# Earlier places for head projections and a dispatch, a root in place of a power, and first rows fetched before their weights, in a two-layer transformer kernel

## The chip, the cores and the metric

The kernel runs on one core of one Trainium2 chip. The metric is the device time of one execution in microseconds (us); lower is better. Before the change three runs took 674.36, 676.66 and 676.97 us, so the median is 676.66 us.

## The reference, cut to what matters

The input is 2048 tokens (8 sequences of 256) of 128 channels, all float32. Six blocks follow one another, each with a residual:

```python
x = x + 0.5 * L0_ffn(layernorm(x))   # mixture of experts, stage f=0
x = x + L0_attn(layernorm(x))        # 16 heads of 8 channels
x = x + 0.5 * L0_ffn(layernorm(x))   # the same mixture, stage f=1
x = x + 0.5 * L1_ffn(layernorm(x))   # channel mix
x = x + L1_attn(layernorm(x))        # gated long convolution
x = x + 0.5 * L1_ffn(layernorm(x))   # channel mix again

def L0_ffn(s):
    h = rmsnorm(s @ W_in.T)
    logits = h @ Wr.T                       # 8 experts
    idx = top_k(logits + expert_bias, 2)    # two experts for each token
    gates = softmax(logits[idx])
    ...
    oe = rmsnorm((silu(h @ Wg[e].T) * (h @ Wu[e].T)) @ Wd[e].T)
    out = sum of gates * oe over the token's two experts
    return rmsnorm(out) @ W_out.T
```

## The kernel before

Tokens lie in four chunks `xs[0..3]` of 512 (four tiles of 128 rows). SP issues plain DMAs, POOL issues the indirect ones.

**A dispatch** sends a group of tokens to its experts. For f=1 there are five, `LATE = (0, 4), (4, 4), (8, 4), (12, 2), (14, 2)` (first tile, number of tiles), numbered 0 to 4 here. Its pieces are `turned` (transpose, PE, and a copy, ACT), `product` twice (`half0`, `half1`: projection to h and logits, then row sums of squares), `measured` (variance of x, DVE), `normed` (1 over the root, `ri`), `logits`, `scaled` (rows of h to `hrow`, ACT), `choice` 0 and 1 (the two best experts, chains of small DVE operations), `places` (a running count by matmuls against a triangle, `prank`, which gives each row its place `posi`), and `rows`: one indirect DMA a tile and choice, from POOL, that writes 128 rows of `hrow` into `hs` in DRAM. Four-tile dispatches have eight such DMAs, two-tile ones four. In f=1 `normed` lets POOL compute the power -0.5 (`power_of`, L144); in f=0 ACT takes the root and DVE the reciprocal (L349, L350).

**The table.** After the last dispatch DVE works out from the counts which expert each of 24 tile turns belongs to (`table`), SP and ACT queue eight DMAs that write zeros behind each expert's rows (`zeros`, L514), and SP then fetches for each turn the expert's weights (`w_f`, L544, 832 KB) and the rows (`hst_f`, L550, 129 KB for 256 rows). Each fetch is preceded by a load of a register from the table. The fetch of rows waits for all writes of `hs`. PE then runs for each turn the transposes of the rows (`pht`), `pg` and `pu` (L566) and, a turn later, `py` (L589). Four weight buffers rotate.

**Attention** stands between the two mixtures. It runs in steps s = 0 to 34, each with two places "a" and "b": s is a sequence and a group of four heads (eight steps a chunk). In each place PE computes weights (`ps`, L910) for one earlier step side by side with scores (`pm`, L893) for the new one; ACT takes the exponentials (`es`), DVE the maxima (`m`). Other work is hung into the places by hand, `at(step, place, pieces)`: the combination of f=0's output for chunk n, its layer norm (`norm_sums`, `norm_rows`), the transposes (`turn_rows`, `pxn_a`), the projections to q and k (`to_heads`, part 0 and part 1, `pqk`, copied to `qkc`), the values, the ends of earlier sequences (`turn_back`, `turn_heads`, `out_heads`), and the dispatches of f=1. `to_heads` part 1 also queues one DMA to DRAM (`heads<-qkc`) and four that bring q and k back with the heads spread over partitions (`qk<-heads`); chunk n's scores begin at step 8n. These side jobs share one PSUM bank, `sa`, so each waits for the reader of the one before. PE, DVE, ACT and SP keep the program's order; POOL's order comes from the scheduler.

Of the kernel before, what the change touches and what calls it, by code (L numbers as in the profile page):

```python
# [11 lines left out]
AF = mybir.ActivationFunctionType  # L12
# [5 lines left out]
B, S, D = 8, 256, 128  # L18
# [4 lines left out]
E, DFF = 8, 512  # L23
# [7 lines left out]
I32 = mybir.dt.int32  # L31
# [8 lines left out]
TURNS = [t for i in range(7) for t in (2 * i, 2 * i + 1, NPAIR + i)] + [14, NPAIR + 7, NPAIR + 8]  # L40
# [6 lines left out]
WALL = 3 * DFF + D  # L47
# [4 lines left out]
def macaron_kernel(ctx: ExitStack, tc: tile.TileContext, a: dict, out: bass.AP):  # L52
    nc = tc.nc
# [32 lines left out]
    rms_eps = const.tile([P, 1], F32, tag="rms_eps", name="rms_eps")  # L86
# [10 lines left out]
    def pack(name, widths, rows=P):  # L97

        t = const.tile([rows, sum(widths)], F32, tag=name, name=name)
        nc.sync.dma_start(t, a[name])  # L100
        cuts, o = [], 0
        for w in widths:
            cuts.append(t[:, o : o + w])
            o += w
        return cuts

    load_x(0)
    win, wr_t, inw, eb, tri, slot, base, order, tokid = pack(
        "pack1", [D, E, 1, E, P, 2, E, E, NCH * TPC * 2]
    )  # L110
    tokid = tokid.rearrange("p (t k) -> p t k", k=2).bitcast(I32)
# [4 lines left out]
    zero = const.tile([P, 2 * ROW], F32, tag="zero", name="zero")  # L116
    nc.vector.memset(zero, 0.0)
    warm = const.tile([P, 1], F32, tag="warm", name="warm")
    nc.scalar.activation(warm, rms_eps, AF.Sqrt)

    hs = tc.dram_tile([HS_ROWS, ROW], F32, name="hs")
    (tabc,) = pack("pack2", [TABLE])
# [176 lines left out]
    def dispatch(f, i, parts, mp):  # L299

        t0, nt = parts[i]
        n = f"f{f}_{i}"
        st = {}
        x = xs[t0 // TPC][:, t0 % TPC : t0 % TPC + nt, :]
        hrow = hrows[t0 // TPC][:, t0 % TPC : t0 % TPC + nt]
        slots = slice(t0, t0 + nt)
# [38 lines left out]
        def normed():  # L345
            ri = small.tile([P, nt], F32, tag="ri", name=f"ri_{n}")
            nc.vector.scalar_tensor_tensor(ri, st["ss"], 1.0 / D, st["z"], ALU.mult, ALU.add)  # L347
            if f == 0:
                nc.scalar.activation(ri, ri, AF.Sqrt)  # L349
                nc.vector.reciprocal(ri, ri)  # L350
                nc.vector.tensor_copy(hrow[:, :, :, D].bitcast(I32), tokid[:, slots])
            else:
                power_of(ri, ri, mhalf.to_broadcast([P, nt]))
            st["ri"] = ri
# [75 lines left out]
        halves, choices = ([partial(p, i) for i in range(2)] for p in (product, choice))  # L430
# [101 lines left out]
    def experts(f, tab, far, y2, mp, pieces):  # L532

        SP = mybir.EngineType.SP
        hst, w, ht, hg = {}, {}, {}, {}
# [4 lines left out]
        def fetch_weights(t):  # L540
            n = f"f{f}_{t}"
            e = nc.values_load(tab[0:1, 1, t : t + 1], engines=[SP], min_val=0, max_val=E - 1)
            w[t] = mp.tile([P, WALL], F32, tag="w", name=f"w_{n}", bufs=4)
            nc.sync.dma_start(w[t], a["wall"][bass.ds(e, 1), :, :].rearrange("o p f -> p (o f)"))  # L544

        def fetch_rows(t):
            n, m = f"f{f}_{t}", blocks(t)
            row = nc.values_load(tab[0:1, 0, t : t + 1], engines=[SP], min_val=1, max_val=HS_ROWS - TT)
            hst[t] = mp.tile([P, 2, ROW], F32, tag="hst", name=f"hst_{n}", bufs=4)[:, 0:m]
            nc.sync.dma_start(hst[t], hs[bass.ds(row, m * P), :].rearrange("(s p) c -> p s c", p=P))  # L550
# [67 lines left out]
                tc.add_to_no_dep_group(f"y2{f}", ins.ins)  # L618

        for t in TURNS[:3]:  # L620
            fetch_weights(t)
            fetch_rows(t)
        turn_rows(TURNS[0])
        for i, t in enumerate(TURNS):
            sg = gate(t)
# [107 lines left out]
    def heads(hp):  # L733
# [26 lines left out]
        def attention(mixing, leaving, filter_ends):  # L760
# [5 lines left out]
            with tc.tile_pool(name="at2", bufs=2, reuse_waits="tile") as a2:  # L766
# [206 lines left out]
                def at(s, h, *pieces):  # L973
                    places_[s, h] += pieces
# [7 lines left out]
                for n in range(1, NCH):  # L982
                    sums, added, turned, produced, update = mixing[n + 1]
                    o = 8 * n - 8
                    if n == 1:
                        at(0, "b", sums)
                        at(1, "b", added)
                        o += 1
                    else:
                        at(o - 1, "b", sums)  # L990
                        at(o, "b", added)
                    at(o + 1, "a", turned)
                    at(o + 1, "b", produced)
                    at(o + 2, "a", update)
                    at(o + 2, "b", partial(norm_sums, n))
                    at(o + 3, "a", partial(norm_rows, n))
                    if n == 1:
                        at(3, "b", seq1[4])
                        o -= 1
                    at(o + 4, "b", partial(turn_rows, n))  # L1000
                    at(o + 5, "a", partial(to_heads, n, part=0))
                    at(o + 5, "b", partial(to_heads, n, part=1))
                    at(o + 8, "a", partial(values, n))
                for b in range(B - 1):
                    o = 4 * b
# [8 lines left out]
                for c in range(2):  # L1014
                    o = 8 * c + 8
                    turned, half0, half1, measured, normed_, logits, scaled, *choices, places, rows = leaving[c]
                    at(o + 4, "a", turned)
                    at(o + 4, "b", measured)
                    at(o + 6, "a", half0)
                    at(o + 8, "b", half1)  # L1020
                    at(o + 9, "a", normed_)
                    at(o + 9, "b", logits, choices[0])
                    at(o + 10, "b", partial(scaled, [0, 1]))
                    at(o + 11, "b", partial(scaled, [2, 3]))
                    at(*((o + 13, "b") if c == 0 else (o + 10, "b")), choices[1])
                    at(*((25, "a") if c == 0 else (27, "b")), places)
                    for i in range(TPC):
                        at((25, 29)[c] + i, "b", partial(rows, [i]))
                turned, half0, half1, measured, normed_, logits, scaled, *choices, places, rows = leaving[2]
                at(28, "b", turned)  # L1030
                at(29, "a", half0)
                at(29, "b", half1, measured)
                at(30, "a", normed_)
                at(31, "a", logits)
                at(31, "b", scaled, choices[0])
                at(32, "b", choices[1])
                at(33, "a", places)
                at(33, "b", rows)
                turned, half0, half1, measured, normed_, logits, scaled, *choices, places, rows = leaving[3]
                t2, h20, h21, measured2, normed2, logits2, scaled2, *choices2, places2, rows2 = leaving[4]  # L1040
                at(32, "a", turned)
                at(32, "b", half0, half1, measured, normed_)
                at(33, "b", logits, scaled, choices[0])
                at(
                    34,
                    "a",
                    partial(turn_back, B - 1),
                    choices[1],
                    partial(turn_heads, B - 1),
                    partial(out_heads, B - 1),  # L1050
                    t2,
                    measured2,
                    places,
                    h20,
                    rows,
                    h21,
                    normed2,
# [431 lines left out]
```

## Time and profile before

The profiled execution took 676.0 us, its span (first to last instruction) is 674.2 us.

| stretch, us | what | PE busy, us | DVE busy, us | POOL busy, us | granted PE clock |
|---|---|---|---|---|---|
| 12 to 50 | dispatches of f=0 | 19.52 of 38 | 24.86 | 20.95 | 1.00 |
| 50 to 68 | table, first fetches | 0.41 of 18 | 7.54 | 9.92 | 1.00 |
| 68 to 188 | experts of f=0 | 114.39 of 120 | 57.95 | 53.75 | 1.00 |
| 188 to 215 | combination of the first tiles | 20.15 of 27 | 9.78 | 5.25 | 0.50 |
| 215 to 396 | attention | 160.90 of 181 | 122.16 | 29.94 | 0.98 |
| 396 to 433 | last dispatches, table, first fetches of f=1 | 6.91 of 37 | 18.08 | 16.24 | 0.58 |
| 433 to 545 | experts of f=1 | 109.35 of 112 | 47.79 | 36.42 | 0.99 |
| 545 to 674 | combination, second layer | 92.17 of 129 | 68.93 | 24.78 | 0.83 |

In a line of the timeline the columns are start, length, engine, source line, operation, output and inputs, and how often; the brackets hold the idle time of the engine just before and what ended it. In the chain of waits each piece released the next.

### The profile page before, as it was taken

The page shows a single profiled execution, that of the slowest core. Times are in us where ns is not written, and L with a number is a line of the kernel's source. Part 1 is how long each engine was busy: PE and PEld are TensorE (multiplying, and loading weights), DVE is VectorE, ACT ScalarE, POOL GpSimd, SP SyncE. Part 2 cuts the span into 40 slices and gives each one's busy share as a digit, 9 for nine tenths or more (in the row PEclk, how much of TensorE's full clock was granted, in tenths as well). Part 3 has the DMA queues.
Part 4 walks back from the last instruction along what each step waited for, and adds up shares of the span by engine and source line. Part 5 has one row for each costly group of instructions (what it writes and reads, how often), then busy time and mean ns, then how long its engine had stood idle before and what let it go on. Part 6 is the DMA issues. An engine that isn't in the chain of part 4 may idle for free. (4 is left out here: it accounts for less than half of the span.)

```text
span 674.2 us, 11485 instructions
## 1 busy us (share of the span) xinstructions
PE 527.5 (78%) x3945; PEld 414.2 (61%) x3945; DVE 360.7 (53%) x1120; ACT 274.4 (41%) x677; POOL 198.0 (29%) x206
## 2 busy tenths in 40 slices
PE   4540999999859888988988971399999925779985
PEld 3530899999835545555555541299899923548864
DVE  4664445544443765748758764344444414756663
ACT  3450233233232665646745640132223315764253
POOL 0475177532431101001005434122333333311000
PEclk9999999999955999999999995599999975889997
DMA  5016577767430321030021101958677731000001
GB/s 207 32 51 165 181 225 218 248 199 231 135 101 0 64 53 13 2 63 1 34 32 33 33 21 49 240 178 239 189 230 233 233 99 43 0 1 1 0 17 47
DMA packets 39753, 69.80 MB, mean 104 GB/s; under 512 B 4939, under 2 KB 30066, under 8 KB 39568
## 3 DMA queue, kind: packets, MB, share of 16 engines
q1 hardware_dynamic: 34000, 59.55, 31.2%
q0 software_dynamic: 4544, 8.47, 3.8%
q10 hardware_dynamic: 1152, 1.06, 0.7%
q8 instruction: 31, 0.51, 0.3%
q14 instruction: 26, 0.21, 0.1%
HBM read 55.60 MB, written 14.38 MB: 104 GB/s over the span
## 5 line engine op out<-in xcount | busy, mean ns | idle before, releaser
L609 POOL DMA_INDIRECT y<-yrow_f,idx_f x78 | 76.5, 981 | 138.6 <-ACT sg_f L575 76.6
L947 ACT ACTIVATE es<-ps 128x1024 f32<-128x1024 f32 x64 | 65.4, 1021 | 57.9 <-PE ps L910 35.7
L420 POOL DMA_INDIRECT hs<-hrow,posi_f x64 | 61.9, 968 | 86.0 <-DVE ri_f L347 35.5
L930 DVE TENSOR_REDUCE m<-pm 128x4 f32<-128x1024 f32 x64 | 77.6, 1221 | 16.4 <-PE pm L893 16.4
L910 PE MATMUL ps<-qa,qk 32*128 32x256 f32 x512 | 74.2, 403 | 14.2 <-ACT es L947 9.7
L893 PE MATMUL pm<-qk 32*128 32x256 f32 x512 | 79.5, 414 | 4.9 <-DMA qk<-heads 3.5
L566 PE MATMUL pg_f<-ht_f,w_f 128*128 128x256 f32 (+1 forms) x384 | 79.3, 351 | 1.2 <-issue 0.6
L589 PE MATMUL py_f<-w_f,hg_f 128*128 128x128 f32 x624 | 78.2, 276 | 2.5 <-DVE yrow_f L600 1.6
L589 PEld LDWEIGHTS py_f<-w_f,hg_f 128*128 128x128 f32 x624 | 75.2, 192 | 4.7 <-DVE yrow_f L600 3.3
L566 PE MATMUL pu_f<-ht_f,w_f 128*128 128x256 f32 (+1 forms) x384 | 76.6, 343 | 0.0
L582 DVE TENSOR_TENSOR hg_f<-pu_f,sg_f 128x1024 f32<-128x1024 f32 (+1 forms) x48 | 49.2, 1024 | 46.3 <-PE pu_f L566 46.1
L575 ACT ACTIVATE sg_f<-pg_f 128x1024 f32<-128x1024 f32 (+1 forms) x48 | 41.4, 863 | 65.6 <-PE pg_f L566 65.6
L566 PEld LDWEIGHTS pg_f<-ht_f,w_f 128*128 128x128 f32 x384 | 63.2, 197 | 7.4 <-issue 1.0
L599 ACT ACTIVATE ysq_f<-py_f 128x128 f32<-128x128 f32 x78 | 21.0, 274 | 109.9 <-PE py_f L589 92.6
L566 PEld LDWEIGHTS pu_f<-ht_f,w_f 128*128 128x128 f32 x384 | 61.5, 193 | 6.0
L910 PEld LDWEIGHTS ps<-qa,qk 32*128 32x128 f32 x512 | 43.5, 184 | 31.1 <-ACT es L947 21.0
L893 PEld LDWEIGHTS pm<-qk 32*128 32x128 f32 x512 | 47.2, 191 | 10.0 <-DMA qk<-heads 6.0
L600 DVE TENSOR_TENSOR yrow_f<-py_f,w_f 128x256 f32<-128x256 f32 (+1 forms) x48 | 18.0, 375 | 53.0 <-ACT ysq_f L599 52.9
L556 PE MATMUL pht_f<-ident,hst_f 128*128 128x128 f32 x78 | 17.3, 286 | 32.7 <-DMA hst_f<-hs 32.7
L558 DVE TENSOR_SCALAR ht_f<-pht_f,pack 128x256 f32<-128x256 f32 (+1 forms) x48 | 20.7, 432 | 40.6 <-PE pht_f L556 39.6
L957 PE MATMUL po<-es,v 128*32 128x256 f32 x512 | 35.1, 393 | 0.0
L144 POOL TENSOR_TENSOR cf_f<-cf_f,mhalf 128x8 f32<-128x8 f32 (+1 forms) x9 | 13.5, 1502 | 66.0 <-DVE cf_f L665 66.0
(257 smaller groups left out, 834.4 us busy)
## 6 DMA issues: line engine op xcount, KB each, us to landing
w_f<-in_wall_dram SPq DMA_DIRECT2D x48, 832.0 KB
hst_f<-hs SPq DMA_DIRECT2D x30, 129.0 KB
y_f<-y SPq DMA_DIRECT2D x14, 258.0 KB
pack<-in_pack_dram SPq DMA_DIRECT2D x1, 1729.0 KB
heads<-qkc SPq DMA_DIRECT2D x3, 512.0 KB
qk<-heads SPq DMA_DIRECT2D x12, 128.0 KB
y<-yrow_f,idx_f POOLq DMA_INDIRECT x78, 5.2
hst_f<-hs SPq DMA_DIRECT2D x18, 64.5 KB
```

The source lines that it names most:

```text
L420: ins = nc.gpsimd.indirect_dma_start(out=hs, out_offset=bass.IndirectOffsetOnAxis(ap=st["posi"][:, t, k : k + 1], axis=0), in_=hrow[:, t, ...
L566: nc.tensor.matmul(ph[:, k, :], w[t][:, o + k * P : o + k * P + P], ht[t], start=True, stop=True)
L575: nc.scalar.activation(sg, pg, AF.Silu)
L582: nc.vector.tensor_mul(hg[t], pu, sg)
L589: nc.tensor.matmul(py[:, s, :], hg[t][:, k, ts(s, P)], w[t][:, 2 * DFF + k * D : 2 * DFF + k * D + D], start=(k == 0), stop=(k == NFC - 1),)
L599: nc.scalar.activation(sq[:, s], py[:, s], AF.Square, accum_out=yrow[:, s, D : D + 1])
L609: ins = nc.gpsimd.indirect_dma_start(out=y2, out_offset=bass.IndirectOffsetOnAxis(ap=idx[:, s : s + 1], axis=0), in_=yrow[:, s, :], in_off ...
L893: nc.tensor.matmul(sc[:, jj, i, :], qs[c][r, g, col + i * P : col + (i + 1) * P], ks[c][r, g, col : col + S], start=True, stop=True,)
L910: nc.tensor.matmul(sc[:, jj, i, :], ks[c][r, g, col + i * P : col + (i + 1) * P], tops[s][r, :], start=True, stop=True,)
L930: nc.vector.tensor_reduce(m, sc, AX.X, ALU.max, negate=True)
L947: nc.scalar.activation(es, sc, AF.Exp, scale=scale)
L957: nc.tensor.matmul(po[32 * j : 32 * j + 32, :], vs[c][:, (b % 2) * 2 + i, (g % 2) * (H // 2) + (g // 2) * 4 + j, :], ess[s, j // 2][:, j % ...
```

## The change

Five edits in one. (1) For chunks 2 and 3 `turn_rows` and both parts of `to_heads` each go one place earlier, so part 1 and its DMAs stand at step o+5 "a" in place of o+5 "b"; the `turned` of dispatches 0 and 1 moves from o+4 "a" to o+5 "b". (2) Dispatch 2 is moved up: `turned` 28 "a" (was 28 "b"), `measured` 28 "b" (29 "b"), `logits` and `choice` 0 30 "b" (31), `choice` 1 31 "b" (32 "b"), `places` 32 "a" (33 "a"), `rows` 32 "b" (33 "b"). Dispatch 3's `turned` goes from 32 "a" to 32 "b" and its next pieces from 32 "b" to 33 "a"; in step 34 `h20`, dispatch 4's projection, now stands before dispatch 3's `places`. (3) The last dispatch, 4, takes ACT's root and DVE's reciprocal in place of POOL's power; a call `root_table` at the head of step 34 brings ACT's table for the root. (4) In f=1 the first three turns ask for rows before weights. (5) Their first turn's weights come in three DMAs (512, 512 and 640 columns). In f=0 a copy of token numbers moves ahead of the root.

In the built program POOL's order near the end of attention was: power for dispatch 2, last row DMA of dispatch 1, power for dispatch 3, eight row DMAs of dispatch 2, four of dispatch 3, power for dispatch 4, four of dispatch 4. It is now: power for dispatch 2, last row DMA of dispatch 1, eight of dispatch 2, power for dispatch 3, four of dispatch 3, four of dispatch 4.

```diff
+    def root_table():
+        nc.scalar.activation(warm, rms_eps, AF.Sqrt)
+
+    root_table()
...
             if f == 0:
+                nc.vector.tensor_copy(hrow[:, :, :, D].bitcast(I32), tokid[:, slots])
+            if f == 0 or i == len(parts) - 1:
                 nc.scalar.activation(ri, ri, AF.Sqrt)
                 nc.vector.reciprocal(ri, ri)
-                nc.vector.tensor_copy(hrow[:, :, :, D].bitcast(I32), tokid[:, slots])
             else:
                 power_of(ri, ri, mhalf.to_broadcast([P, nt]))
...
-            nc.sync.dma_start(w[t], a["wall"][bass.ds(e, 1), :, :].rearrange("o p f -> p (o f)"))
+            wall = a["wall"][bass.ds(e, 1), :, :].rearrange("o p f -> p (o f)")
+            ends = (0, DFF, 2 * DFF, WALL) if f and t == TURNS[0] else (0, WALL)
+            for o, end in zip(ends, ends[1:]):
+                nc.sync.dma_start(w[t][:, o:end], wall[:, o:end])
...
         for t in TURNS[:3]:
-            fetch_weights(t)
-            fetch_rows(t)
+            for fetch in (fetch_rows, fetch_weights) if f else (fetch_weights, fetch_rows):
+                fetch(t)
...
-                    at(o + 4, "b", partial(turn_rows, n))
-                    at(o + 5, "a", partial(to_heads, n, part=0))
-                    at(o + 5, "b", partial(to_heads, n, part=1))
+                        at(4, "b", partial(turn_rows, n))
+                        at(5, "a", partial(to_heads, n, part=0))
+                        at(5, "b", partial(to_heads, n, part=1))
+                    else:
+                        at(o + 4, "a", partial(turn_rows, n))
+                        at(o + 4, "b", partial(to_heads, n, part=0))
+                        at(o + 5, "a", partial(to_heads, n, part=1))
...
-                    at(o + 4, "a", turned)
                     at(o + 4, "b", measured)
+                    at(o + 5, "b", turned)
...
-                at(28, "b", turned)
+                at(28, "a", turned)
+                at(28, "b", measured)
                 at(29, "a", half0)
-                at(29, "b", half1, measured)
+                at(29, "b", half1)
                 at(30, "a", normed_)
-                at(31, "a", logits)
-                at(31, "b", scaled, choices[0])
-                at(32, "b", choices[1])
-                at(33, "a", places)
-                at(33, "b", rows)
+                at(30, "b", logits, choices[0])
+                at(31, "b", scaled, choices[1])
+                at(32, "a", places)
+                at(32, "b", rows)
...
-                at(32, "a", turned)
-                at(32, "b", half0, half1, measured, normed_)
+                at(32, "b", turned)
+                at(33, "a", half0, half1, measured, normed_)
                 at(33, "b", logits, scaled, choices[0])
                 at(
                     34,
                     "a",
+                    root_table,
                     partial(turn_back, B - 1),
                     choices[1],
...
                     measured2,
+                    h20,
                     places,
-                    h20,
                     rows,
```

More of the change, by code (lines that the diff above doesn't have):

```diff
@@ L118, in macaron_kernel @@
     warm = const.tile([P, 1], F32, tag="warm", name="warm")
-    nc.scalar.activation(warm, rms_eps, AF.Sqrt)
+    def root_table():
+        nc.scalar.activation(warm, rms_eps, AF.Sqrt)
+    root_table()
     hs = tc.dram_tile([HS_ROWS, ROW], F32, name="hs")
```

## The prediction

> **What bounds the kernel now.** I read the page's slices first: PE is busy 78% of the span, so I looked for the stretches where it is not, and in those for the last wait to end.
>
> The waits of PE inside attention (engine and line that waited, for whom, total us, times, longest):
>
> ```profile
> PE pm L893 <- DMA qk<-heads: 3.5, 3, 1.5
> ```
>
> The timeline shows where: at steps 8, 16 and 24, when scores turn to a new chunk. These are steps 16 and 24, which the change touches, with what follows the first:
>
> ```profile
> 302.20 0.48 PE L893 MATMUL pm<-qk 32*128 32x256 f32 x1 [1.48 <-DMA qk<-heads]
> 303.31 1.94 PE L957 MATMUL po<-es,v 128*32 128x256 f32 x16
> 305.17 1.28 PE L333 MATMUL pin_f<-win_r,xnt_f 128*128 128x136 f32 x4
> 306.38 0.56 PE L910 MATMUL ps<-qa,qk 32*128 32x256 f32 x2
> ...
> 348.12 0.48 PE L893 MATMUL pm<-qk 32*128 32x256 f32 x1 [1.14 <-DMA qk<-heads]
> 350.84 0.48 PE L910 MATMUL ps<-qa,qk 32*128 32x256 f32 x2
> ```
>
> The reader is to see two costs: the idle time (1.48 and 1.14 us) and, after the first, `po` at 1.94 us (1.07 elsewhere) and `pin` at 1.28 (0.73 at 350.18): the windows view has the clock at 0.50 from 304 to 306.
>
> Then the end of attention, POOL's timeline first, with DVE's line that waited for it:
>
> ```profile
> 394.27 0.76 POOL L144 TENSOR_TENSOR ri_f<-ri_f,mhalf 128x2 f32<-128x2 f32 x1 [12.17 <-DVE cnt_f L404]
> 396.80 1.04 POOL L420 DMA_INDIRECT hs<-hrow,posi_f  x1 [1.78 <-ACT osb L966]
> ...
> 410.78 0.96 POOL L420 DMA_INDIRECT hs<-hrow,posi_f  x1 [0.31 <-issue]
> 411.76 0.72 POOL L144 TENSOR_TENSOR ri_f<-ri_f,mhalf 128x2 f32<-128x2 f32 x1
> 412.52 0.18 DVE L358 TENSOR_TENSOR lg_f<-u_f,ri_f 128x16 f32<-128x16 f32 x1 [7.37 <-POOL ri_f L144]
> 418.80 1.03 POOL L420 DMA_INDIRECT hs<-hrow,posi_f  x1 [6.32 <-issue]
> ```
>
> Dispatch 4's power (411.76) stands behind twelve row DMAs at 1.26 us each (396.80 to 411.74); its input was ready at 405.15. All engines but POOL wait. Dispatch 3's power (394.27) ran before these rows.
>
> Last, the chain of waits (start, length, what released the next):
>
> ```profile
> 422.68 6.79 DMA hs<-hrow,posi_f
> ...
> 429.66 2.09 DMA hst_f<-hs
> ...
> 433.13 3.53 PE pg_f L566 x8
> ```
>
> The last row DMA lands 6.79 us after its start and holds the first fetch of rows; in the first mixture the last one started at 62.01 and the fetch went at 65.29, 3.28 us. The difference here: the first weights (832 KB) were asked for at 424.89, and zeros are in flight.
>
> [...]
>
> **The change part by part**, against the profiled 676.0 us (span 674.2 plus 1.8 around it; 0.7 below the median).
>
> *Heads of chunks 2 and 3.* `qkc`'s second copy ran at 287.15, its first at 284.00; part 1 takes the slot of part 0, so the DMAs start 3.1 us earlier (chunk 3: 333.22 against 330.08). Both stalls are shorter: −1.48 −1.14. The inputs are there: `xn_a` ends at 275.39, the moved transposes come at 277.97. PE's places trade a 0.6 us transpose for a 1.0 us projection and back, which cancels. The slow window goes too: from the end of the stall to the next `ps` chunk 2 took 4.18 us, chunk 3 with the same pieces 2.72, so −1.46. Sum −4.1; [...]−4.5 if smaller waits go along.
>
> *Dispatches at the end of attention.* Followed in times of before. `logits` and `choice` 0 of dispatch 2 now follow `cc` (ends 383.46) and take 1.68 us (357.28 to 358.96), which holds the next `qa`, so PE's next weights start at about 385.6 (before 384.80). `choice` 1 ends at about 390.1, `prank` 1.3 us later (before 393.76 to 395.07), the cast of `posi` 0.95 later, POOL 0.78 later (396.02 to 396.80). Taking off 0.4 for a transpose that moves into PE's 0.80 us gap in step 28: rows of dispatch 2 start at about 392.8, 4.0 earlier.
>
> But dispatch 3's power now stands behind these eight rows: 392.8 + 8 x 1.26 = 402.9, less 0.3 after the last, plus 0.75 gives 403.3. DVE sits in `lg` of dispatch 3, which began at 395.93 before: 7.5 us later. Queued behind it on DVE are `choice` 0 and 1 of dispatch 3, `cc` of the last sequence and so the last output heads, x and dispatch 4. From `lg` to the end of dispatch 4's transposed copy (401.37) it took 5.4: 408.8. [...]`pcc`, `pwo`, `pxt` (0.41 + 0.71 + 0.44) run at about half rate: +1.1, 409.9. `pin` 1.28 and `u` 0.45: 411.6. `prank` of dispatch 3 waits for that copy, since both use bank `sa`, then takes 1.47 (415.54 to 417.01) at half rate: 413.1. From `at_row` to `posi` 0.85: 414.0. Root and reciprocal, `ri` to `lg`, take about 0.57 in the first mixture (24.20 to 24.85 less a copy of 0.1): `lg` of dispatch 4 at 414.6, against 412.52. So the edit that saves 6.6 us of POOL's queue is paid by the move of dispatch 2: +2.1. Ends: +0.4 (fast clock, no wait for the bank), +3.3 (attention loses another us to the choices).
>
> The table load of the root (1.28 us in the row of L575) stands between `hrow` of dispatch 3 and `ct`, some 2.0 us apart, so nothing[...]. The load for the exponential back again lies beside the table on DVE (ACT idle 13.07 us): nothing.
>
> *Rows before weights.* With no weights in flight the last rows can land at best 2.3 us after their instruction, as in the first mixture (62.97 to 65.29): 423.65 + 2.3 = 425.95. The zeros still drain; I take 427.3, so −2.3 of 429.66 (−3.7 to −1.0).
>
> *Weights in pieces.* The first piece (256 KB) goes 1.19 us after the rows (429.66 to 430.85) and needs about what the rows need, 2.09: 3.3 after the rows' issue, where `pg` starts at 3.47: +0.2 (0 to +1). SP issues two more DMAs of 0.37 us; the second turn's weights go at about +4.4 instead of +1.19 and are needed at +8.78 (438.44); at 352 GB/s (434 to 438) 832 KB take 2.4[...]: hidden[...].
>
> *Clock at the start of the experts.* `pg` took 3.53 and then full speed; in the first mixture 3.75 and a slow `pu` of 2.66 followed, 1.15 worse. [...]: +0.5 (0 to +1.7).
>
> *The copy in f=0*: 0.1 us on DVE five times, beside POOL's rows that run to 62.97: nothing.
>
> Sum: −4.1 + 2.1 − 2.3 + 0.2 + 0.5 = −3.6, so 672.4 in the profile's terms, 673.1 from the median. I say 672.8.
>
> **Rivals.** *Full gain (0.10)*: POOL is through with dispatch 2 before dispatch 3 asks, so the root's 6.6 us stay and the dispatches give −6 in place of +2.1: about 664.5. For it: POOL's gap of 12.17 us ahead of 394.27. Against: the ready time of dispatch 3's sum (393.95) lies after the rows' new start.
>
> *Heads gain little (0.15)*: PE's places are held by `es` (9.7 us in 21 waits), and what the stall frees is lost there; the edit gives −1: about 676. Against: at both boundaries DVE also idles over 2 us.
>
> *Slower (0.15)*: the weight stream becomes the experts' bound. It starts at 424.89 now; behind the rows it starts 2.1 + 1.2 + 427.3 − 424.89 = 5.7 later, less 4.1 from attention is +1.6, with the clock's 0.5 about 678.5. 24 loads of 832 KB at 222 GB/s are 90 us of the 112. It decides if PE waits over 3 us in all for `w_f` in the experts; before it idled 2.65 of 112 us.
>
> **How the numbers follow.** The forecast has 0.60, its own range 670 to 675.5. What a measurement of this kernel can tell from no change is about 0.5%, 3.4 us, so the border is 673.3; the forecast splits 0.40 faster, 0.20 the same. Full gain adds 0.10 to faster, small gain 0.15 to the same, the stream 0.05 to the same and 0.10 to slower. The range 668.5 to 677.0 leaves out most of the first and last.
>
> **What would show it.** No PE wait for `qk<-heads` at steps 16 and 24 and one fewer slow window; dispatch 3's power right behind eight rows, with DVE idle about 6 us before its `lg`; root and reciprocal within 0.6 us; under 5 us from the last row DMA to the fetch of rows; `pg` within 4 us of that fetch. I am wrong if DVE's wait is short, if PE waits for weights in the first three turns, or if the attention stretch doesn't shorten by 3 us.

## The result, and the profile after

| kernel | median us | range, runs | ratio to before, 95% interval |
|---|---|---|---|
| before | 676.71 | 674.36 to 681.16, 12 | |
| after | 673.76 | 672.48 to 675.7, 12 | 0.9965, 0.9948 to 0.9982 |

The change makes the kernel 0.35% faster, by the ratio 2.4 us (1.2 to 3.5). The profiled execution of after took 675.26 us, its span is 673.5: near the slow end of its runs, so the pair of profiles shows where time moved better than how much of it stayed.

PE's waits inside attention, after (engine and line that waited, for whom, total us, times, longest):

```profile
PE pm L901 <- DMA qk<-heads: 1.1, 1, 1.1
```

Two of three waits are gone; the one left is at step 8, which the change doesn't touch. PE's timeline around steps 16 and 24 of after:

```profile
300.60 1.07 PE L965 MATMUL po<-es,v 128*32 128x256 f32 x16
301.60 0.73 PE L337 MATMUL pin_f<-win_r,xnt_f 128*128 128x136 f32 x4
302.26 0.48 PE L918 MATMUL ps<-qa,qk 32*128 32x256 f32 x2
...
344.05 0.73 PE L337 MATMUL pin_f<-win_r,xnt_f 128*128 128x136 f32 x4
344.71 0.48 PE L918 MATMUL ps<-qa,qk 32*128 32x256 f32 x2
```

`po` and `pin` of step 16 took 1.07 and 0.73 us at a granted clock of 1.00 (1.94 and 1.28 in before, at 0.50), and the first `ps` behind them comes at 302.26 (before 306.38), that of step 24 at 344.71 (before 350.84): 4.1 and 6.1 us earlier, of which 0.9 were there before attention's first `ps` (217.87 against 218.73). Attention as a whole, from that `ps` to the last `pm`, takes 163.67 us in place of 166.84: after step 24 it loses again part of what it had won.

The end of attention in after, timeline of POOL, DVE and ACT:

```profile
388.37 0.96 POOL L425 DMA_INDIRECT hs<-hrow,posi_f  x1 [11.12 <-issue]
...
394.60 0.16 DVE L351 SCALAR_TENSOR_TENSOR ri_f<-ss_f,z_f 128x2 f32<-128x2 f32 x1 [6.19 <-ACT sqin_f L345]
...
397.21 0.96 POOL L425 DMA_INDIRECT hs<-hrow,posi_f  x1 [0.30 <-issue]
398.18 0.73 POOL L148 TENSOR_TENSOR ri_f<-ri_f,mhalf 128x2 f32<-128x2 f32 x1
398.95 0.17 DVE L363 TENSOR_TENSOR lg_f<-u_f,ri_f 128x16 f32<-128x16 f32 x1 [4.19 <-POOL ri_f L148]
...
409.44 0.15 DVE L351 SCALAR_TENSOR_TENSOR ri_f<-ss_f,z_f 128x2 f32<-128x2 f32 x1
409.63 0.20 ACT L355 ACTIVATE ri_f<-ri_f 128x2 f32<-128x2 f32 x1 [1.75 <-DVE ri_f L351]
409.87 0.17 DVE L356 RECIPROCAL ri_f<-ri_f 128x2 f32<-128x2 f32 x1 [0.27 <-ACT ri_f L355]
410.07 0.17 DVE L363 TENSOR_TENSOR lg_f<-u_f,ri_f 128x16 f32<-128x16 f32 x1
```

The rows of dispatch 2 start at 388.37 (before 396.80). Dispatch 3's sum of squares is ready at 394.60, but its power stands behind the eighth row, and `lg` of dispatch 3 comes at 398.95: 3.0 later than before, although the last `pm` of attention started 4.0 us earlier (381.54 against 385.57). The last dispatch has its `lg` 0.63 us after its sum (7.5 before), and yet only 2.45 us earlier (410.07 against 412.52).

The first fetches of the second mixture in after, timeline of SP and PE, with the last row DMA ahead of them:

```profile
420.30 0.97 POOL L425 DMA_INDIRECT hs<-hrow,posi_f  x1 [0.30 <-issue]
...
425.65 0.41 SPq L558 DMA_DIRECT2D hst_f<-hs  x1
426.86 1.46 SPq L552 DMA_DIRECT2D w_f<-in_wall_dram  x3
...
429.61 3.75 PE L574 MATMUL pg_f<-ht_f,w_f 128*128 128x256 f32 x8 [0.99 <-DMA w_f<-in_wall_dram]
...
433.58 2.82 PE L574 MATMUL pu_f<-ht_f,w_f 128*128 128x256 f32 x8
```

The fetch of rows goes 5.35 us after the last row DMA's start (6.98 before). The first `pg`, 3.5 us earlier than before, waits a last 0.99 us for its piece of the weights, and the `pu` behind it took 2.82 us, with the granted clock at 0.50 up to 435.0. PE's waits in the experts of after:

```profile
PE pg_f L574 <- DMA w_f<-in_wall_dram: 2.7, 3, 1.0
```

Before had none on `w_f`. The three waits are in the first turn (0.99), the fifth (0.72) and a later one (0.95). In this profile the 3.5 us are gone by the last `py`: 543.79 against 543.71.

### The profile page after: what moved, and what is told of

Same layout as the page of the kernel before. It is cut to its first block, busy times and chain, and to the rows that moved or that the text cites. A ratio compares the mean times of both kernels' runs of the same rounds, so it can differ in the third digit from the quotient of the medians.

```text
span 673.5 us, 11493 instructions
## 1 busy us (share of the span) xinstructions
PE 532.8 (79%) x3945; PEld 416.5 (62%) x3945; DVE 361.3 (54%) x1121; ACT 277.4 (41%) x681; POOL 197.2 (29%) x205
## 5 line engine op out<-in xcount | busy, mean ns | idle before, releaser
L965 PE MATMUL po<-es,v 128*32 128x256 f32 x512 | 36.8, 408 | 0.0
```

Of the source, the lines that this page charges most:

```text
L965: nc.tensor.matmul(po[32 * j : 32 * j + 32, :], vs[c][:, (b % 2) * 2 + i, (g % 2) * (H // 2) + (g // 2) * 4 + j, :], ess[s, j // 2][:, j % ...
```

## Experiments

Each kernel was timed against the kernel before in runs on the same chip. The chips differ: before took 678.7 us beside e1 to e4, 699.2 beside e5 to e8, 698.2 beside e9 to e12. So only ratios are compared, and differences in us are the ratio's deviation from 1 times that median. The last pm of attention starts at 381.5 to 389.1 us in the profiles of the faster chips and at 400.3 to 409.0 on the others, so the chips differ ahead of the end of attention; starts after it are given against it. This table is worked out from the timelines, starts minus the start of the last `pm`, us:

| kernel | `lg`, dispatch 3 | `lg`, dispatch 4 | last row DMA | fetch of rows | first `pg` | last `py` |
|---|---|---|---|---|---|---|
| before | 10.36 | 26.95 | 37.11 | 44.09 | 47.56 | 158.14 |
| after | 17.41 | 28.53 | 38.76 | 44.11 | 48.07 | 162.25 |
| e1 | 10.36 | 26.94 | 37.09 | 44.83 | 48.43 | 161.26 |
| e2 | 17.41 | 28.55 | 38.80 | 46.81 | 50.41 | 161.61 |
| e3 | 10.36 | 26.98 | 37.14 | 43.00 | 47.03 | 160.05 |
| e4 | 14.44 | 25.60 | 36.10 | 42.47 | 46.56 | 157.87 |
| e5 | 10.36 | 22.08 | 32.15 | 37.79 | 43.11 | 156.16 |
| e6 | 17.42 | 28.54 | 38.79 | 44.59 | 50.35 | 161.73 |
| e7 | 10.36 | 20.97 | 31.44 | 39.42 | 44.62 | 155.91 |
| e8 | 10.34 | 20.97 | 32.21 | 37.29 | 41.40 | 152.17 |
| e9 | 17.42 | 28.55 | 38.80 | 41.47 | 45.47 | 159.01 |
| e10 | 17.42 | 28.56 | 38.81 | 44.63 | 48.21 | 159.47 |
| e11 | 10.36 | 26.93 | 37.09 | 43.55 | 47.14 | 160.54 |
| e12 | 10.36 | 22.01 | 32.09 | 38.59 | 42.48 | 152.98 |

**e1: the heads alone**, against before.

```diff
-                    at(o + 4, "b", partial(turn_rows, n))
-                    at(o + 5, "a", partial(to_heads, n, part=0))
-                    at(o + 5, "b", partial(to_heads, n, part=1))
...
+                    else:
+                        at(o + 4, "a", partial(turn_rows, n))
+                        at(o + 4, "b", partial(to_heads, n, part=0))
+                        at(o + 5, "a", partial(to_heads, n, part=1))
...
-                    at(o + 4, "a", turned)
+                    at(o + 5, "b", turned)
```

> The kernel before with the first part of the change alone: the heads of chunks 2 and 3 and their turned rows one place earlier, all else as before. Theory (the heads' arrival was what PE waited for at steps 16 and 24[...]): 4 to 5.5 us faster than before, about 672, ratio 0.992 to 0.994, with no wait of PE for the heads at steps 16 and 24, and a start of dispatch 4 some 4 us earlier. Rival A (the stalls go, but something later in attention or in the last dispatches takes the time back): within 1 us of before. Rival B (the parts of the change add up by simple sums, and the whole gain of 2.95 is from the heads): 2.5 to 3.5 us faster.

Measured: 674.23 against 678.71 us, ratio 0.9933 (0.9908 to 0.9959), 4.5 us faster (2.8 to 6.2). PE's waits in attention of e1, then of e2, which keeps the old places:

```profile
PE pm L893 <- DMA qk<-heads: 1.5, 3, 1.0
```

```profile
PE pm L898 <- DMA qk<-heads: 4.4, 4, 1.5
```

The timeline has 1.01 us of e1's waits at step 8 and 0.24 and 0.25 at two other places: the stalls at steps 16 and 24 are gone. The theory holds and rival A falls. Rival B's 2.5 to 3.5 us are within the interval; e2 and e3 decide on it.

**e2: the dispatches and the root alone**, against before; heads and fetches stay.

```diff
+            if f == 0 or i == len(parts) - 1:
...
-                at(31, "b", scaled, choices[0])
-                at(32, "b", choices[1])
-                at(33, "a", places)
-                at(33, "b", rows)
+                at(30, "b", logits, choices[0])
+                at(31, "b", scaled, choices[1])
+                at(32, "a", places)
+                at(32, "b", rows)
...
```

> The kernel before with the moves of the last dispatches and the root and reciprocal of the last norm alone; heads and first fetches as before. Theory (the root saves dispatch 4 the stretch that its power spent behind twelve rows on POOL, but dispatch 3's power now stands behind the eight rows of dispatch 2, and what comes after it on DVE is late by as much): 0 to 2 us slower than before, with lg of dispatch 3 some 7 us later and lg of dispatch 4 some 2 us later than before on the same start of attention. Rival (the power that is gone from the last dispatch was the whole of the wait, so dispatch 4 ends earlier): 4 to 6 us faster. Second rival (the dispatch end isn't what the experts wait for): within 0.5 us.

Measured: 681.77, ratio 1.0034 (1.0014 to 1.0054), 2.3 us slower (1.0 to 3.7). POOL and DVE of e2:

```profile
404.77 0.96 POOL L425 DMA_INDIRECT hs<-hrow,posi_f  x1 [0.30 <-issue]
405.75 0.72 POOL L148 TENSOR_TENSOR ri_f<-ri_f,mhalf 128x2 f32<-128x2 f32 x1
...
406.50 0.18 DVE L363 TENSOR_TENSOR lg_f<-u_f,ri_f 128x16 f32<-128x16 f32 x1 [6.47 <-POOL ri_f L148]
...
417.64 0.17 DVE L363 TENSOR_TENSOR lg_f<-u_f,ri_f 128x16 f32<-128x16 f32 x1
```

DVE stands still 6.47 us for a power of 0.72 us that had to let the eight rows pass. Against the last `pm`, `lg` of dispatch 3 is 7.05 later, `lg` of dispatch 4 1.6 later, the last row DMA 1.7 later: the theory's numbers, and both rivals fall.

**e3: the first fetches alone**, against before.

```diff
-            nc.sync.dma_start(w[t], a["wall"][bass.ds(e, 1), :, :].rearrange("o p f -> p (o f)"))
+            ends = (0, DFF, 2 * DFF, WALL) if f and t == TURNS[0] else (0, WALL)
+            for o, end in zip(ends, ends[1:]):
+                nc.sync.dma_start(w[t][:, o:end], wall[:, o:end])
...
-            fetch_weights(t)
-            fetch_rows(t)
+            for fetch in (fetch_rows, fetch_weights) if f else (fetch_weights, fetch_rows):
+                fetch(t)
```

> The kernel before with the first fetches of the second expert layer alone: rows asked for ahead of their weights, and the first turn's weights in three pieces. Theory (the first fetch of rows stood 2.3 us behind the weights' issue, and the first turn of matmuls starts that much earlier; some of it is lost again to a wait for the weights in the second turn): 1 to 2.5 us faster than before. Rival (the later weights become the experts' bound: what the first turn wins, the next turns wait): within 0.5 us of before, PE waiting for w_f 2 us or more in all, last py at the same time after the last row's landing as before. Slower by over 1 us if the first turn itself waits for its weights.

Measured: 678.39, ratio 1.0002 (0.9982 to 1.0021), 0.1 us slower (1.2 faster to 1.4 slower). The fetch of rows goes 5.86 us after the last row DMA, against 6.98, 7.74 and 8.01 in before, e1 and e2; the first `pg` comes 9.89 after it, against 10.45 to 11.61. So about a us is won at the first `pg`, and the median of the whole doesn't show it. The theory's least gain of 1 us is inside the interval; of the rival's waits there are 1.2 us for `w_f`, not 2. This run alone leaves it open; below it is taken up over all profiles.

The three parts add up: −4.5 + 2.3 + 0.1 = −2.1 us, where the whole change measured −2.4. Rival B of e1, that the heads alone make the gain, falls with that: they give nearly twice as much, and the dispatches take half of it back.

**e4: the root for dispatch 3 too**, against after.

```diff
-            if f == 0 or i == len(parts) - 1:
+            if f == 0 or i >= len(parts) - 2:
...
-                at(33, "a", half0, half1, measured, normed_)
+                at(33, "a", half0, root_table, half1, measured, normed_)
...
-                    root_table,
```

> The changed kernel, with the root and reciprocal for dispatch 3 too, and the load of the root's table moved from step 34 to step 33 ahead of it. Theory (dispatch 3's power behind the eight rows on POOL is what keeps the end of the dispatches late): lg of dispatch 3 about 2.8 us earlier than in the changed kernel (within 2.5 us of its sum of squares instead of 4.2 behind it), and the whole 1.5 to 3 us faster than the changed kernel, about 671, ratio against before 0.991 to 0.994. Rival (the late power only filled time in which POOL's rows or PE's work of the last steps set the end, or the table's load now stands in ACT's way in steps 33 and 34): within 0.7 us of the changed kernel, ratio 0.9955 to 0.9975.

Measured: 672.6, ratio 0.9912 (0.9885 to 0.994), 6.0 us faster than before (4.1 to 7.8). Its interval ends below that of after (0.9948). DVE and POOL of e4:

```profile
394.44 0.16 DVE L351 SCALAR_TENSOR_TENSOR ri_f<-ss_f,z_f 128x2 f32<-128x2 f32 x1 [5.76 <-ACT sqin_f L345]
396.04 0.17 DVE L356 RECIPROCAL ri_f<-ri_f 128x2 f32<-128x2 f32 x1 [1.45 <-ACT ri_f L355]
396.24 0.19 DVE L363 TENSOR_TENSOR lg_f<-u_f,ri_f 128x16 f32<-128x16 f32 x1
...
407.40 0.17 DVE L363 TENSOR_TENSOR lg_f<-u_f,ri_f 128x16 f32<-128x16 f32 x1
...
417.90 0.99 POOL L425 DMA_INDIRECT hs<-hrow,posi_f  x1 [0.30 <-issue]
```

`lg` of dispatch 3 comes 1.80 us after its sum (4.35 in after), and against the last `pm` both `lg` and the last row DMA are 2.7 to 3.0 us earlier than in after, the fetch of rows and the first `pg` 1.6 and 1.5. The power behind the rows was the cost; the rival falls.

**e5: the root alone**, against before, dispatches in the places of before.

```diff
-            if f == 0:
+            if f == 0 or i == len(parts) - 1:
...
                     34,
                     "a",
+                    root_table,
                     partial(turn_back, B - 1),
```

> The kernel before with the root and reciprocal of the last norm alone, and the load of the root's table; the dispatches stay in the places of before, so dispatch 3's power stays ahead of the eight rows of dispatch 2. Theory (what the root saves was eaten in the change by the move of dispatch 2): lg of dispatch 4 0.7 us after its sum of squares instead of 5.5 to 7.5, the four rows of dispatch 4 directly behind the other twelve on POOL or at most 2.2 us later, the last row DMA 5 to 6.8 us earlier against the last pm of attention (30.3 to 32.1 us after it instead of 37.1), and the whole 4.5 to 6.5 us faster than before, ratio 0.990 to 0.9935. Rival (POOL's row DMAs or the table of places bound the end, not the norm): last row DMA at most 1 us earlier and the whole within 1 us.

Measured: 695.63 against 699.21, ratio 0.9942 (0.9923 to 0.996), 4.1 us faster (2.8 to 5.4). PE, DVE and POOL of e5, from the last `pm` on:

```profile
409.00 0.38 PE L898 MATMUL pm<-qk 32*128 32x256 f32 x2
...
430.37 0.23 DVE L351 SCALAR_TENSOR_TENSOR ri_f<-ss_f,z_f 128x2 f32<-128x2 f32 x1 [1.83 <-ACT sqin_f L345]
431.08 0.18 DVE L363 TENSOR_TENSOR lg_f<-u_f,ri_f 128x16 f32<-128x16 f32 x1
...
441.15 0.96 POOL L425 DMA_INDIRECT hs<-hrow,posi_f  x1 [0.30 <-issue]
```

`lg` of dispatch 4 comes 0.71 us after its sum, as the theory said, and 4.9 us earlier against the last `pm` than in before; the last row DMA comes 5.0 us earlier (32.15 against 37.11), a hair outside the theory's 30.3 to 32.1. The gain in time lies below its 4.5 to 6.5. The rival falls. In e7, e8 and e12, with the same edit, the last row DMA is at 31.4 to 32.2.

**e6: the first weights whole**, against after.

```diff
-            ends = (0, DFF, 2 * DFF, WALL) if f and t == TURNS[0] else (0, WALL)
-            for o, end in zip(ends, ends[1:]):
-                nc.sync.dma_start(w[t][:, o:end], wall[:, o:end])
+            nc.sync.dma_start(w[t], a["wall"][bass.ds(e, 1), :, :].rearrange("o p f -> p (o f)"))
```

> The changed kernel with the first turn's weights of the second expert layer in one transfer again, still behind the rows. Theory (the pieces let the first matmuls start on a third of the weights): the first pg 1 to 2 us later behind the fetch of rows than the 4.0 us of the changed kernel, all of it a wait for w_f, and 0.5 to 2 us slower than the changed kernel, ratio against before 0.997 to 1.0. Rival (the whole transfer lands in the time of a piece, or the next turns' weights come earlier by as much, since SP issues two transfers fewer): within 0.5 us of the changed kernel or faster.

Measured: 698.33, ratio 1.0005 (0.9978 to 1.0033), against 0.9965 for after. PE of e6:

```profile
450.68 3.75 PE L571 MATMUL pg_f<-ht_f,w_f 128*128 128x256 f32 x8 [2.79 <-DMA w_f<-in_wall_dram]
```

`pg` starts 5.76 us after the fetch of rows in place of 3.96, all of it the longer wait (2.79 for 0.99). Once rows go first, the pieces are worth 1.8 us at that place. By the ratios e6 is 2.7 us slower than after, more than the theory's 0.5 to 2, but the intervals of the two kernels overlap by a hair, so the size in time is open.

**e7: heads and root, without the other three parts.** e1's and e5's edits together.

```diff
+                        at(o + 4, "a", partial(turn_rows, n))
+                        at(o + 4, "b", partial(to_heads, n, part=0))
+                        at(o + 5, "a", partial(to_heads, n, part=1))
...
+            if f == 0 or i == len(parts) - 1:
```

> The kernel before with the heads' part and with the root of the last norm, dispatches in the places of before, first fetches as before. Theory (the two gains are in different stretches and add up): 9 to 11 us faster than before, ratio 0.984 to 0.987, faster than the changed kernel by 6 us or more. Rival (they overlap, or the root alone wins little because POOL's rows bound the end): 4 to 6 us faster, as the heads alone.

Measured: 690.11, ratio 0.9879 (0.9839 to 0.9918), 8.5 us faster than before (5.7 to 11.3); e1 and e5 sum to 8.6. It lies just short of the theory's 0.984 to 0.987, and clear of after's interval. DVE of e7, then SP:

```profile
421.15 0.16 DVE L351 SCALAR_TENSOR_TENSOR ri_f<-ss_f,z_f 128x2 f32<-128x2 f32 x1 [1.79 <-issue]
421.78 0.17 DVE L363 TENSOR_TENSOR lg_f<-u_f,ri_f 128x16 f32<-128x16 f32 x1
...
429.15 0.36 DVE L457 TENSOR_TENSOR tab_over<-tab_cnt,pack 128x64 f32<-128x64 f32 x2 [1.39 <-DVE tab_first L451]
430.59 0.29 DVE L461 TENSOR_REDUCE tab_num<-tab_over 128x16 f32<-128x128 f32 x1 [1.07 <-DVE tab_over L457]
432.74 0.29 DVE L466 TENSOR_REDUCE tab_cum<-tab_over 128x16 f32<-128x128 f32 x1 [1.19 <-DVE tab_over L464]
```

```profile
438.88 0.35 SPq L549 DMA_DIRECT2D w_f<-in_wall_dram  x1
440.23 0.41 SPq L555 DMA_DIRECT2D hst_f<-hs  x1
```

The whole 6 us at `lg` of dispatch 4 and 5.7 at the last row DMA arrive. Then the next bound shows: DVE works out the table after that, here with stalls between its own operations, and the first weights are asked for only 1.35 us ahead of the rows (4.77 in before).

**e8: e7 with the change's first fetches.** This is after less the moves of dispatches 2 to 4.

```diff
-            fetch_weights(t)
-            fetch_rows(t)
+            for fetch in (fetch_rows, fetch_weights) if f else (fetch_weights, fetch_rows):
+                fetch(t)
```

> As the kernel with heads and root, and with the change's first fetches too (rows ahead of their weights, these in pieces). So it is the changed kernel less the move of dispatches 2 to 4. Theory (the rows come 1.7 us sooner, pg starts 1.2 us sooner, and waits for weights in the first turns and the clock give it back): within 1 us of the kernel without the fetch part. Rival (the first fetch is on the path and its gain stays): 1.2 to 2.5 us faster than that one. Rival two (the weights bound the experts): slower than it by over 1 us, PE waiting over 2 us for w_f.

Measured: 690.45, ratio 0.9894 (0.9858 to 0.9931), beside e7's 0.9879. The theory's "within 1 us" fits, but with intervals of 2.5 us on each side either rival could be true as well: inconclusive in time. PE waited 1.1 us for `w_f`, not the over 2 of rival two. In the profile its fetch of rows comes 2.1 us ahead of e7's and its `pg` 3.2, but 1.6 of that is the table: DVE came to its end (`tab_free`) 37.4 us behind the last `pm`, in e7 39.0.

**e9: no zeros in the second mixture**, against after. The rows that pad a tile keep what the first mixture left there.

```diff
-        zeros(f, first)
+        if f == 0:
+            zeros(f, first)
```

> The changed kernel without the zero rows that the second mixture writes behind each expert's rows (the rows that pad a tile keep what the first mixture left there, so that part of the output isn't computed as before). Theory[...]: the fetch of rows goes 3.0 to 4.0 us after the last row DMA's start instead of 5.35 to 6.4, and the whole is 1 to 2.5 us faster than the changed kernel, ratio against before 0.9925 to 0.995. Rival (the wait is the rows' own landing or the table of places): the fetch still 5 us or more after the last row DMA's start, and no gain.

Measured: 693.39 against 698.17, ratio 0.9911 (0.9881 to 0.9941), 6.2 us faster than before (4.1 to 8.3), some 3.8 more than after, where the theory said 1 to 2.5. POOL and SP of e9:

```profile
442.82 0.98 POOL L425 DMA_INDIRECT hs<-hrow,posi_f  x1 [0.30 <-issue]
...
445.49 0.39 SPq L559 DMA_DIRECT2D hst_f<-hs  x1
```

SP's wait for the rows in after, and then the only wait of SP in e9 around these fetches (counted from SP's work before, 102 us earlier):

```profile
SPq L558 <- DMA hs<-hrow,posi_f: 2.7, 1, 2.7
```

```profile
SPq L557 <- DVE tab_room L500: 102.2, 1, 102.2
```

It took 2.67 us from the last row DMA to the fetch (the theory said 3.0 to 4.0), where after has 5.35. That is after's figure less its wait of 2.7 us; in e9 SP doesn't wait for the rows at all, and the table is what the fetch waits for. So with the zeros in flight they, and not the rows alone or the table, hold the fetch back by 2.7 us once the weights go behind the rows. The rival falls. In what way they hold it back isn't shown: the zeros write `hs` too, and e9 can't tell a late landing of the rows from the zeros' own.

**e10: the first piece of the weights ahead of the rows, the rest behind**, against after.

```diff
+            if f and t == TURNS[0]:
+                fetch_weights(t, 0)
+                fetch_rows(t)
+                fetch_weights(t, 1)
+                continue
             for fetch in (fetch_rows, fetch_weights) if f else (fetch_weights, fetch_rows):
                 fetch(t)
```

> The changed kernel with the first turn's weights in two parts around its rows: the part for the gate (256 KB) ahead of the fetch of rows, the other two behind it. Theory (it is the size of the weights in flight that held the rows back, and the wait for the first piece that cost the change a us at its first pg): the fetch of rows 5.3 to 6.2 us after the last row DMA's start, no wait of the first pg for w_f, pg 3.4 to 3.7 us after that fetch; the whole 0 to 1 us faster than the changed kernel. Rival (any weights ahead of the rows hold them back as in the kernel before): the fetch 7 us or more behind the last row DMA's start, as before, and the whole up to 1.5 us slower than the changed kernel.

Measured: 694.23, ratio 0.9946 (0.9924 to 0.9969), not to be told from after. SP and PE of e10:

```profile
441.60 0.97 POOL L425 DMA_INDIRECT hs<-hrow,posi_f  x1 [0.30 <-issue]
...
443.87 0.35 SPq L556 DMA_DIRECT2D w_f<-in_wall_dram  x1
447.42 0.41 SPq L562 DMA_DIRECT2D hst_f<-hs  x1
...
451.00 3.75 PE L578 MATMUL pg_f<-ht_f,w_f 128*128 128x256 f32 x8 [0.58 <-DVE ht_f L570]
```

The fetch is 5.82 us behind the last row DMA and `pg` 3.58 behind the fetch, with no wait for weights: the theory's figures. A piece of 256 KB ahead of the rows holds them back no more than can be seen (5.82 lies within the 5.35 to 6.37 of after, e3 and e4). From the last row DMA to `pg` it took 9.40 us; after has 9.31, e3 and e4 9.89 and 10.46. The theory's gain can't be told from the spread between profiles, and the rival falls.

**e11: the heads of chunk 2 alone**, against before. The `turned` of dispatch 0 moves with them, as in the change.

```diff
+                    if n != 2:
                         at(o + 4, "b", partial(turn_rows, n))
                         at(o + 5, "a", partial(to_heads, n, part=0))
                         at(o + 5, "b", partial(to_heads, n, part=1))
+                    else:
+                        at(o + 4, "a", partial(turn_rows, n))
+                        at(o + 4, "b", partial(to_heads, n, part=0))
+                        at(o + 5, "a", partial(to_heads, n, part=1))
```

> The kernel before with the heads of chunk 2 alone one place earlier; chunk 3 as before. By the terms of the prediction (1.48 of stall and 1.46 of slow clock at step 16, 1.14 at step 24) this has 2.9 of the 4.1 us: ratio about 0.9957, PE's waits for heads 1.4 to 1.5 us less than the 3.5 to 4.4 of the kernels with the old places, with the wait at step 24 still there. Rival (a slow window follows step 24's stall as well, or simply comes at another place, so that the chunks count about alike): 1.5 to 2.2 us faster, ratio 0.9967 to 0.998, a slow window of the clock at another step of attention.

Measured: 694.56, ratio 0.9942 (0.9915 to 0.997), 4.0 us faster (2.1 to 5.9). PE of e11, its waits for heads:

```profile
265.29 0.48 PE L893 MATMUL pm<-qk 32*128 32x256 f32 x1 [1.07 <-DMA qk<-heads]
...
307.51 0.48 PE L893 MATMUL pm<-qk 32*128 32x256 f32 x1 [0.16 <-DMA qk<-heads]
352.19 0.48 PE L893 MATMUL pm<-qk 32*128 32x256 f32 x1 [0.74 <-DMA qk<-heads]
```

Of the stall at step 16 0.16 us are left, at step 24 0.74 stay. The theory's 2.9 lies in the interval, the rival's 1.5 to 2.2 only at its edge: chunk 2 carries most of the gain, by the medians. How much is left for chunk 3 these intervals can't say. The rival's sign, a slow stretch later in attention, is there (a granted clock down to 0.50 from 365 to 368.5 and from 371.5 to 389), but all profiles on the slower chips, e5 to e12, have stretches at 0.50 between 359.5 and 400, so it decides nothing.

**e12: e7's kernel once more, on another chip.**

> The kernel with heads and root alone once more, on the chip of these runs. In its first profile DVE stood still five or six times in the table of places (4.6 us in all, 12 us from the counts to the table's last row instead of 7.4), with zeros and fetches behind it. Theory (this comes of the row DMAs that follow each other on POOL without a pause up to the table): the same stalls again, the fetch of rows 7.5 to 9 us behind the last row DMA, ratio against before 0.985 to 0.989. Rival (it was that chip or that execution): no stalls, the fetch of rows 6 to 7 us behind the last row DMA and 3 us earlier against the last pm, ratio 0.981 to 0.985.

Measured: 692.68 against 698.17, ratio 0.9902 (0.9863 to 0.9941). DVE's waits in the table of e12 (who waited, for whom, total us, times, longest):

```profile
DVE tab_single L490 <- DVE tab_room L488: 0.7, 1, 0.7
DVE tab_cum L466 <- DVE tab_over L464: 0.3, 1, 0.3
DVE tab_odd L484 <- DVE tab_odd L483: 0.3, 1, 0.3
```

From `tab_cnt` to `tab_free` it took 9.0 us (12.3 in e7, 7.4 in after). There are stalls again, so the rival's "none" is wrong, but they are at other operations and come to 1.5 us in place of 4.8; the fetch of rows is 6.50 us behind the last row DMA, which is the rival's figure, but against the last `pm` only 0.8 earlier than in e7, not 3, and the ratio's interval reaches into the theory's range and not into the rival's. So stalls came in both executions of this kernel, and their size differed. The profiled execution, 686.40 us, was the fastest of e12's nine (686.40 to 693.97), so it may understate the stalls of the others. What makes them isn't settled.

## Why the prediction was right

The forecast, 672.8 us, is 1 us from the median of 673.76. That closeness flatters it: its gain of 3.9 us lies outside the measured 1.2 to 3.5. The direction and the terms of the heads and the dispatches were right; the term of the fetches was too large. By its own terms:

- *Heads, −4.1.* e1 measured −4.5 (−6.2 to −2.8), and both stalls are gone. The clock's share, −1.46, was put down to one slow stretch behind step 16's stall, and that isn't shown. Between 230 and 380 us before and after have one stretch of 3.5 to 4 us each with the granted clock down to 0.50 (from 303 and 353.5). With the old places e2 has two (303.5 and 361.5) and e3 two (259.5 and 362); with the new ones e1 has one (355), e4 none. That is about one less over the six, but not always the one that was counted. In e3 the stall of 1.10 us at step 8 was followed by such a stretch and that of 1.38 at step 16 was not (1.00 from 263.5 to 362); why one comes isn't settled.
- *Dispatches and root, +2.1.* e2 measured +2.3. Each step came in: rows of dispatch 2 earlier, the power behind the eight rows, `lg` of dispatch 3 7.05 later (7.5 said), `lg` of dispatch 4 1.6 later (2.1 said), root and reciprocal 0.63 (0.6 said). DVE's idle time of 6 us is 6.47 in e2 and 4.19 in after, where dispatch 3's own sum came some 2 us later, with the granted clock at 0.50 from 388 on (PE was busy 7.32 of the 8 us up to 396). At that clock `pcc`, `pwo` and `pxt` took 0.66, 1.23 and 0.69 us in after (0.41, 0.71 and 0.44 in before), +1.0 where +1.1 was estimated. Rival "full gain" failed on the ready time of that sum, as written; e7 gets its 6 us at `lg` of dispatch 4 by leaving dispatch 2 where it was.
- *Table loads, nothing.* In after the load of 1.28 us stands between 399.87 and 401.15 and ACT still has 0.8 us to spare before the next copy at 402.15.
- *Rows before weights, −2.3.* This term was mis-sized. Against the last row DMA the fetch moved from 6.98 to 8.01 (before, e1, e2) to 5.35 to 6.37 (after, e3, e4): 1.7 on the means (7.58 and 5.86). With e11 (6.46) and e6 (5.80), whose dispatches end as in before and in after, it is 1.45 (7.30 and 5.85). "Under 5 us" failed. The prediction allowed the zeros 1.35 us (427.3 against 425.95); e9 shows 2.7 for them, from 5.35 down to 2.67, more than the weights' 1.5 to 1.7. What transfers in flight would cost the rows was the author's estimate; what makes the rows land later isn't shown.
- *Weights in pieces, +0.2, and clock, +0.5.* `pg` starts 3.96 after the fetch (3.47 before): +0.5. The first `pu` took 2.82 in after and 1.89 in before, at a mean granted clock of 0.67 and 1.00; but it took 2.81 in e5, where weights go first, and 2.12 in e4, so this difference isn't tied to the order of the fetches. The clock's term was the author's estimate from the first mixture, where `pg` and `pu` took 3.75 and 2.66 at a granted clock of 1.00 (68 to 75), so the clock isn't shown to be what made them slow there. From the last row DMA to `pg` the mean is 9.89 (after, e3, e4) against 11.13 (before, e1, e2), or 10.86 with e11: −1.0 to −1.2 where −1.6 was counted up to the end of the slow `pu`. e3 measured +0.1 (−1.2 to +1.4).
- *The weight stream as the bound.* PE waited 2.7 us for `w_f` in after, near the 3 us set as the mark. Over all profiles, the stretch from the first `pg` to the last `py` is 110.8 to 114.2 us, mean 112.0, in the six kernels with rows first and zeros (after, e3, e4, e6, e8, and e10 with one piece ahead), and 110.5 to 113.4, mean 111.8, in the seven with weights first (before, e1, e2, e5, e7, e11, e12): no sign that the stream took the place of the rows. After's own 114.2 is the longest of all, so its profile overstates what was lost there.
- *The signs.* Those at steps 16 and 24, of the power behind the rows and of `pg` within 4 us came true. "One fewer slow window" didn't in the pair of before and after, and one sign of being wrong came true: PE waited 0.99 us for weights in the first turn. The attention stretch shortened by 3.2 us, just over the 3 that were set.

The sum was −3.6 where −2.4 was measured by the ratio (−2.95 between the medians). What is missing is in the fetches: −1.6 was counted for them, and the parts measured −4.5, +2.3 and +0.1. Why the 1.0 to 1.2 us won at the first `pg` doesn't show in e3's median isn't settled; its interval still allows it.

The lowest ratio is e7's: 0.9879 and 0.9902 on two chips, against 0.9965 for the change, with both intervals below the change's. It isn't told apart from e8 (0.9894), from e9 (0.9911) or from e4, the change with a second root (0.9912), whose intervals overlap with its own.

## What to carry to other kernels

In e2 DVE stood still 6.47 us for a power of 0.72 that ran on POOL behind eight row DMAs: ask of every piece moved up which short operation of another chain it now stands in front of. Taking the short operation off that engine (e5, and e4 against after) won 4.1 and 3.6 us, while moving the long ones ahead (e2) turned the same saving into a loss. When a transfer waits for "all writes", look at every writer in flight and not only at the one that the change moves: here the zeros held the fetch back longer (2.7 us) than the weights that were taken out of its way (1.5 to 1.7).

## What the runs showed of the hardware that was not expected

- Eight writes of zeros, 129 KB each, cost the following read 2.7 us (e9 against after); an 832 KB load of weights ahead of it cost 1.5 to 1.7 on the means.
- Chips differ by 3% on the same program (676.7 and 678.7 against 698.2 and 699.2 us), nearly all ahead of the end of attention: after and e10 are the same program up to there, and their last `pm` starts at 381.54 and 402.79. In e10 the granted clock went down to 0.50 in three stretches between 362 and 393.5, 22 us in all, where after has one of 3.5 us between 230 and 387; what makes the chips differ isn't shown.
- In e12 twelve row DMAs follow each other on POOL and the last four begin 3.04 us after the start of the twelfth; there DVE stands still between its own dependent small operations in the table for 1.5 us, and in e7, the same program, for 4.8. In before and after, where POOL pauses for 6.32 and 11.40 us among these rows, no wait of DVE inside the table is longer than 0.3. A cause wasn't shown.
